# Fused attention and gated FFN block in fp32 on one core: late weights loaded behind the first move of queries, the planner's view of an x load in pieces, and the last pair's norm on ACT and DVE

## The chip, the cores and the metric

One core of a Trainium2 chip runs the whole kernel. The metric is the device time of one execution in microseconds; the figure of a kernel is the median of its runs. The engines are TensorE (PE: matmuls, and transposes done as matmuls), VectorE (DVE), ScalarE (ACT), GpSimd (POOL) and SyncE (SP). SP issues nearly all DMAs here, in order: an issue that waits holds up all behind it. An L with a number is a line of the kernel before.

## What is computed

x has 4096 rows of 256 numbers, all fp32. A block of windowed attention (16 query heads in 4 groups, head size 16, each row sees the 128 rows up to itself) and a gated feed-forward block (with a mix of each row and the row before it) follow each other, each with a residual and a layer norm:

```python
q = x @ Wq + bq;  k = x @ Wk + bk;  v = x @ Wv + bv      # k, v: 4 groups of 16
mask = (i - 128 >= j) | (i < j)
att = softmax(where(mask, -1e9, q @ k.T / sqrt(16)))
x = layernorm(x + (att @ v) @ Wo + bo)
x_prev = concat([0, x[:-1]])
xr = mu_r * x + (1 - mu_r) * x_prev
xk = mu_k * x + (1 - mu_k) * x_prev
r = sigmoid(xr @ W_r.T);  k = xk @ W_k.T
out = r * (square(relu(k)) @ W_v.T)
x = layernorm(x + out)
```

## The kernel before, in words

**Tiling.** The rows are 32 blocks of 128. Two blocks are a pair p (16 pairs), four blocks a chunk c (8 chunks of 512 rows). Projections run by chunk, attention and feed-forward by pair. x is wanted with its columns on the partitions. For pairs 0 to 3 x is loaded as it is (256 KB, L439) and turned on PE; from pair 4 on it is loaded in four pieces of 64 KB (`load_x_turned`, L453) laid out so that DVE can turn it in squares of 32 (L459). Buffer ring `x` has four places, so pair 4 takes that of pair 0.

**Before the loop.** The function first issues, on SP, x of pairs 0 and 1, Wk, Wv, Wq, x of pairs 2 and 3, then the weights of the feed-forward block W_k, W_r, W_v (L481), Wo in four parts (L502), bo (L507), and mu_r and mu_k (L527). Then come constants and the first transposes of x on PE (L619).

**Attention.** For a chunk: `kv` (L730), two query products `q` (L778) with a copy each on ACT (L789), and `q move` (L800): four DMAs from SBUF to SBUF that bring the odd heads' queries to the partitions of the even ones. All score products read what it moves. `vT` (L753) transposes the values; `ones` (L764) is a small DMA that fills rows of kT. For a pair: `maxima` (L855 with masks L833 and L842) are score products of which DVE takes row maxima (L865); these are turned and sent by four small DMAs (`nm put`, L879) into the queries; `weights a` and `weights b` (L942 with masks L914, L928) are the score products anew, transposed, with the maximum subtracted, and ACT takes their exponentials (L979, L1013); `values` (L1040, L1053) multiplies with v; then `wo` (L1180), the addition of the residual `xres` (loaded in L1165, bo added on POOL in L1171), and the norm.

**Feed-forward.** `fk` (L1296), relu on ACT (L1306), square on POOL (L1310), `fr` (L1323) with the gate on ACT (L1337), `fv` (L1323), then the gating product (L1350), the residual (L1355) and the norm: bn_stats and bn_aggr on DVE (L1118, L1119), four small operations on POOL for the scale (L1124 to L1130), apply on ACT (L1136). The last pair, 15, goes in two halves of 128 rows (`plan_last`, L1383 to L1419): product, gating, residual, statistics and apply on DVE, the power that gives the scale on POOL (L1409). The residual addition of pair 14 is on DVE, of the others on POOL.

**What sets the order.** All operations behind the prologue go through `Plan`. `op` records engine, length, a rank (the kind's own from the table `KINDS`, plus a base that grows with the pair) and what is read and written; `run` then simulates all engines with these lengths and writes the instructions out in the order of the simulated starts. On each engine it takes, among the operations that could start within 0.35 of the earliest, that with the lowest rank. PE is an exception: the table `ORDER` fixes its list by position (0, 1, 2, ...), whatever the simulation says. In it the transposes of W_k, W_r and W_v (`w`, L666) stand at positions 29, 30 and 10. What the prologue loads enters the plan as `given`, of no length, with a landing time written by hand; `begin sp` and the like stand for the prologue's own time on each engine. `QUEUE` holds the time a kind takes of the DMA queue in the simulation. The planner's figures set the order alone; on the chip an instruction starts when its semaphores allow.

In the simulation the four pieces of an `x load` share a buffer, so pieces 1 to 3 depend on piece 0, the taker of the buffer:

```python
deps.update(self.taker[k] for k in uses if k in self.taker)
```

and they could start only when it had landed in the simulation. On the chip they write different partitions and don't wait for each other.

Of the kernel before, what the change touches and what calls it, by code (L numbers as in the profile page):

```python
# [8 lines left out]
F32 = mybir.dt.float32  # L9
# [11 lines left out]
P = 128  # L21
NG = 4
# [16 lines left out]
    "begin pool": (POOL, 5.3, -536.56),  # L39
    "begin sp": (SP, 8.0, -360.66),  # L40
    "w": (PE, 0.43, 0),
    "w copy": (ACT, 0.62, 0.22),
    "x load": (SP, 0.5, -0.16),
    "x turn": (DVE, 0.7, 28.13),
# [43 lines left out]
    "y2 last": (DVE, 0.42, -24.81),  # L88
    "stats last": (DVE, 1.1, 59.97),
    "scale last": (POOL, 0.8, -21.85),  # L90
    "apply last": (DVE, 0.46, -51.24),
    "fv": (PE, 1.72, 0),
# [13 lines left out]
QUEUE = {  # L106
    "x load": 0.45, "x1 in": 0.45, "q move": 1.6, "xres": 1.3, "x1 out": 1.3, "store": 1.3,
}
# [103 lines left out]
class Plan:  # L212
# [20 lines left out]
    def op(self, kind, base, fn, r=(), w=(), uses=(), new=(), banks=(), mode=None, late=None):  # L233

        i = len(self.ops)
        eng, length, rank = KINDS[kind]
        n = self.count[kind] = self.count.get(kind, -1) + 1
        rank = ORDER[kind][n] if eng == PE and ORDER else rank + base  # L240
        deps = set()
        for k in r:
            if k in self.writer:
                deps.add(self.writer[k])
            self.readers.setdefault(k, []).append(i)
        for k in w:
            if k in self.writer:
                deps.add(self.writer[k])
            deps.update(self.readers.pop(k, ()))
            self.writer[k] = i  # L250
        deps.discard(i)
        for k in list(uses) + [key for _, key in new] + [key for key, _ in banks]:
            self.users.setdefault(k, []).append(i)
        deps.update(self.taker[k] for k in uses if k in self.taker)
        for ring, key in new:
            self.taker[key] = i
            ring.queue.append(key)
        for key, _ in banks:
            self.taker[key] = i
        if late is None:  # L260
            late = self.LAND if eng == SP else 0.0
        self.ops.append((eng, length, rank, fn, deps, list(new), list(banks), mode, late, QUEUE.get(kind, 0.1 if eng == SP else 0.0)))

# [3 lines left out]
    def run(self):  # L267
# [42 lines left out]
        while cand:  # L310
# [24 lines left out]
            cand.remove(i)  # L335
            eng, length, _, fn, _, new, banks, mode, late, q = ops[i]
            for ring, key in new:
# [14 lines left out]
            for k in nexts[i]:  # L352
                hop = 0.0 if ops[k][0] == eng and not late else self.DRAIN if eng == PE else self.HOP
                if ops[k][0] == PE and eng == PE:
                    hop = 0.0
                ready[k] = max(ready[k], end[i] + hop)
                left[k] -= 1
                if not left[k]:
                    cand.add(k)
# [7 lines left out]
def postln_block(  # L367
# [63 lines left out]
    def ring(tag, bufs=2):  # L431
        return rings.setdefault(tag, Ring(bufs))
# [63 lines left out]
    ffn_l = {"r": wl_r, "k": wl_k, "v": wl_v}  # L496
    for k, w in (("k", W_k), ("r", W_r), ("v", W_v)):
        load_w(ffn_l[k], w)

    wo = const.tile([P, 2, D], F32, tag="wo", name="wo")  # L500
    for g in range(NG):
        nc.sync.dma_start(  # L502
            out=wo[32 * g : 32 * (g + 1), :, :],
            in_=Wo[64 * g : 64 * (g + 1), :].rearrange("(rp x) n -> x rp n", x=32),
        )
    bo_b = const.tile([P, D], F32, tag="bo_b", name="bo_b")
    nc.sync.dma_start(out=bo_b, in_=bo.partition_broadcast(P))  # L507

# [4 lines left out]
    vecs = const.tile([P, NV], F32, tag="vecs", name="vecs")  # L513
    muT = const.tile([P, 2, C2], F32, tag="muT", name="muT")
    with nc.allow_non_contiguous_dma(reason="small vectors, once"):
# [5 lines left out]
        for o in range(2):  # L521
# [3 lines left out]
            )  # L525
        for w, mu in enumerate((mu_r, mu_k)):
            nc.sync.dma_start(out=muT[:, w, :], in_=mu.rearrange("(p c) -> p c", c=C2))  # L527

# [153 lines left out]
    def plan_load(p):  # L682
# [4 lines left out]
        else:  # L687
            op("given", p, lambda: None, w=[("x", p)], new=[(ring("x", 4), ("x", p))], late=(3.7, 4.5, 7.0, 7.8)[p])

# [598 lines left out]
    def plan_k(p, base):  # L1288
# [19 lines left out]
        def square():  # L1308
            kact[p] = sb.tile([P, C2, H2], F32, tag="kact", name=f"kact_{p}")
            nc.gpsimd.tensor_tensor(kact[p].rearrange("p o n -> p (o n)"), st["kr"], st["kr"], ALU.mult)  # L1310

        op("fk", base, product, r=[("xm", 1, p, 0), ("xm", 1, p, 1), ("w", "k")], w=[key], uses=[("xmt", 1, p)], new=[(ring("kr"), ("krt", p))], banks=[(key, 1)], mode="full")
        soon = base - (60 if p == NP - 1 else 0)
        op("relu", soon, relu, r=[key], w=[("kr", p)], uses=[key, ("krt", p)])
        op("square", soon, square, r=[("kr", p)], w=[("kact", p)], uses=[("krt", p)], new=[(ring("kact"), ("kactt", p))])

# [59 lines left out]
    def plan_last(p, b, base):  # L1376
# [14 lines left out]
        def gated():  # L1391
# [3 lines left out]
            nc.vector.scalar_tensor_tensor(y, sig[p][:, b, :], 1.0, bank(key)[:, 0:D], ALU.add, ALU.mult)  # L1395

        def rest():
            y = y2s[p][:, b, :]
            nc.vector.tensor_tensor(y, y, x1[p][:, b, :], ALU.add)
# [3 lines left out]
            nc.vector.bn_aggr(st["mv"], s6)  # L1403
            nc.vector.tensor_scalar(st["mv"][:, 1:2], st["mv"][:, 1:2], EPS, None, ALU.add)

        def scale():
            ve = st["mv"][:, 1:2]
            st["rstd"] = small.tile([P, 1], F32, tag="rstd_last", name=f"rstd_last_{b}")
            nc.gpsimd.tensor_tensor(st["rstd"], ve, nhalf[:, 0:1], ALU.pow)  # L1409

        def apply():
            if not b:
                res[p] = sb.tile([P, 2, D], F32, tag="res", name=f"res_{p}")
            nc.vector.tensor_scalar(
                res[p][:, b, :], y2s[p][:, b, :], st["mv"][:, 0:1], st["rstd"], ALU.subtract, ALU.mult
            )
# [9 lines left out]
        op("y2 last", base, gated, r=[key, ("sig", p)], w=[("y2a", p, b)], uses=[key, ("sigt", p), y2t])  # L1426
        op("stats last", base, rest, r=[("y2a", p, b), ("x1", p, b)], w=[("y2", p, b)], uses=[y2t, ("x1t", p)])
        op("scale last", base, scale, r=[("y2", p, b)], w=[("rstd", p, b)])
# [7 lines left out]
    for p in range(NP):  # L1436
        c, h = divmod(p, 2)
        plan_load(p)
        if p == 1:
            for k, t in (("k", 9.5), ("r", 10.5), ("v", 11.3), ("wo", 12.0), ("bo", 12.5), ("mu", 13.5)):  # L1440
                op("given", 0, lambda: None, w=[("rest", k)], late=t)
            op("given", 0, lambda: None, w=[("wq",)], late=7.4)
# [13 lines left out]
        plan_v(c, b0)  # L1456
        if c == 0:
            for i, (k, scale) in enumerate((("k", 1.0), ("r", 1.0), ("v", 0.5))):
                plan_weight(k, i, scale)
# [54 lines left out]
```

## Time and profile before

| | us |
|---|---|
| median of 3 runs (345.37 to 349.35) | 346.02 |
| the profiled execution, device time | 345.45 |
| its span, first to last instruction | 343.7 |
| mean granted clock of TensorE | 0.986 |
| first real product (L778) starts | 6.83 |
| last matmul ends | 336.7 |
| last apply on DVE ends (L1414) | 340.80 |
| last store issued on ACT's queue (L1419) | 340.84 |

A line of the chain gives start, duration, engine and line of the work that ended last, followed back from the end; SPq is SP's queue issuing a DMA. A line of the timeline gives start, duration, engine, line, operation, output and inputs, and the number of instructions. A line of a stretch gives PE's busy time, the clock it was granted (1.00 is full), the mean share of the 16 DMA engines that was busy, and GB/s. The waits name who waited for what: total us, times, longest.

### The profile page before, as it was taken

To read this page: it belongs to the slowest core of one execution; us is meant where nothing else is said; L and a number is where in the kernel's file an instruction comes from. 1 tells how busy PE (TensorE), PEld (TensorE's weight loads), DVE (VectorE), ACT (ScalarE), POOL (GpSimd) and SP (SyncE) were. 2 spreads that over 40 slices of the span, in tenths; PEclk is the share of its full clock that TensorE was granted. 3 is DMA by queue.
4 is the path that set the end of the run, shared out by engine and by line. 5 is a ranking of instruction groups with operands and counts; after the bars stand their busy time and mean duration, and the time that the engine had idled before them with its cause. 6 is when DMAs were issued, how large, how long until landed. Compare 5 with 4: busy or idle time off the path is not lost.

```text
span 343.7 us, 11149 instructions
## 1 busy us (share of the span) xinstructions
PE 331.5 (96%) x4729; PEld 221.7 (64%) x4729; DVE 268.9 (78%) x494; ACT 165.8 (48%) x227; POOL 124.8 (36%) x220
## 2 busy tenths in 40 slices
PE   8899999999999999999999999999999999999991
PEld 6455566655765676567666656767767676678871
DVE  7067787778888859999789998698948897678675
ACT  2402554556337583272442645653762386834541
POOL 5200000111404334161326231427632765648773
PEclk9969999999999999999999999999999999999998
DMA  6842333121511243211123220322221224210002
GB/s 191 226 100 47 75 78 68 35 67 19 139 33 35 69 89 94 67 33 58 42 60 98 63 68 32 65 82 84 55 87 41 65 70 120 79 49 31 32 31 92
DMA packets 55062, 24.65 MB, mean 72 GB/s; under 512 B 40644, under 2 KB 54852, under 8 KB 55012
## 3 DMA queue, kind: packets, MB, share of 16 engines
q1 hardware_dynamic: 54832, 23.81, 26.3%
q8 instruction: 37, 0.61, 0.8%
q10 hardware_dynamic: 180, 0.13, 0.1%
q14 instruction: 13, 0.11, 0.1%
HBM read 13.64 MB, written 7.86 MB: 63 GB/s over the span
## 4 chain that ended last, share of the span: by engine, by line
PE 83%; DVE 7%; SPq 3%; POOL 2%; issue 1%; DMA 1%; ACT 1%; POOLq 0%; DVEq 0%
PE ps L1323 14%; PE ps L942 12%; PE ps L855 9%; PE ps L1040 8%; PE ps L1180 8%; PE ps L778 8%; PE ps L1296 7%; PE ps L1053 4%; PE ps L730 4%; PE ps L842 2%; PE ps L914 2%; DVE xm L1268 2%; SPq L800 2%; DVE nm L865 1%; PE ps L753 1%
## 5 line engine op out<-in xcount | busy, mean ns | idle before, releaser
L865 DVE TENSOR_REDUCE nm<-ps 128x6 f32<-128x960 f32 (+1 forms) x96 | 94.7, 1037 | 16.6 <-PE ps L855 15.0
L979 ACT ACTIVATE prA<-ps 128x1024 f32<-128x1024 f32 x64 | 63.2, 1024 | 56.7 <-PE ps L914 53.1
L942 PE MATMUL ps<-qT,kT 17*64 17x512 f32 (+1 forms) x1024 | 54.7, 499 | 0.0
L855 PE MATMUL ps<-kT,qT 16*128 16x160 f32 x1024 | 48.8, 309 | 2.4 <-DMA qT<-qT 2.3
L1124 POOL TENSOR_SCALAR ve_y<-mv_y 128x2 f32<-128x2 f32 x31 | 8.0, 257 | 96.2 <-DVE mv_y L1119 95.3
L855 PEld LDWEIGHTS ps<-kT,qT 16*128 16x128 f32 x1024 | 39.5, 188 | 4.6 <-DMA qT<-qT 3.3
L1268 DVE SCALAR_TENSOR_TENSOR xm<-xd,muT,x1T 128x256 f32<-128x256 f32 x64 | 36.1, 614 | 5.4 <-POOL xd L1260 4.3
L1013 ACT ACTIVATE prB<-ps 128x1024 f32<-128x1024 f32 x32 | 31.0, 1021 | 13.7 <-PE ps L914 12.7
L1260 POOL TENSOR_TENSOR xd<-x1T 128x512 f32<-128x512 f32 x16 | 16.6, 1040 | 43.8 <-DVE x1T L459 43.8
L1065 DVE STREAM_TRANSPOSE oN<-ps 128x1024 f32<-128x1024 f32 x16 | 20.0, 1248 | 15.5 <-PE ps L1053 15.4
L1180 PE MATMUL ps<-wo,attT 128*128 128x256 f32 x128 | 31.4, 388 | 0.3 <-ACT prA L979 0.2
L778 PE MATMUL ps<-xT,wq 128*128 128x512 f32 x64 | 31.2, 612 | 0.3 <-DVE wq L631 0.3
L1040 PE MATMUL ps<-prA,vA 128*32 128x256 f32 x512 | 30.9, 382 | 0.4 <-ACT prA L979 0.2
L1296 PE MATMUL ps<-xm,wkT 128*128 128x256 f32 x128 | 30.8, 383 | 0.0
L1323 PE MATMUL ps<-wrT,xm 128*128 128x256 f32 x128 | 30.8, 383 | 0.0
L1118 DVE BATCH_NORM_STATS2 st_y<-y 128x6 f32<-128x256 f32 x62 | 25.3, 408 | 6.2 <-POOL y L1355 5.6
L942 PEld LDWEIGHTS ps<-qT,kT 17*64 17x64 f32 x1024 | 19.6, 130 | 15.5 <-issue 7.7
L1355 POOL TENSOR_TENSOR y<-y,x 128x512 f32<-128x512 f32 x14 | 19.1, 1364 | 28.0 <-DVE y L1350 27.9
L1323 PE MATMUL ps<-wvT,kact 128*128 128x256 f32 x120 | 29.0, 385 | 0.2
L1171 POOL TENSOR_TENSOR xres<-xres,bo_b 128x512 f32<-128x512 f32 x16 | 20.3, 1271 | 23.1 <-DMA xres<-in_L_attn_x 20.1
L1323 PEld LDWEIGHTS ps<-wrT,xm 128*128 128x128 f32 x128 | 23.8, 190 | 5.2 <-issue 1.6
L1180 PEld LDWEIGHTS ps<-wo,attT 128*128 128x128 f32 x128 | 23.3, 190 | 4.9 <-ACT prA L979 1.1
(109 smaller groups left out, 478.1 us busy)
## 6 DMA issues: line engine op xcount, KB each, us to landing
xres<-in_L_attn_x SPq DMA_DIRECT2D x16, 256.0 KB
out<-res SPq DMA_DIRECT2D x15, 256.0 KB
x1d<-x SPq DMA_DIRECT2D x14, 256.0 KB
x1w<-x1d SPq DMA_DIRECT2D x56, 64.0 KB
x<-in_L_attn_x SPq DMA_DIRECT2D x48, 64.0 KB
qT<-qT SPq DMA_DIRECT2D x32, 64.0 KB
x<-in_L_attn_x SPq DMA_DIRECT2D x4, 256.0 KB
qT<-nmT SPq DMA_DIRECT2D x64, 4.0 KB
```

Of the source, the lines that this page charges most:

```text
L778: nc.tensor.matmul(ps, wq[:, ch, rp, :, :].rearrange("p g x -> p (g x)"), xT[c][:, ch, :], start=(ch == 0), stop=(ch == C2 - 1),)
L855: nc.tensor.matmul(sc[g // 2][:, g % 2, u * W : (u + 1) * W], qT[c][g0 : g0 + DH, (2 * p + j) % NB, s, :, :, :].rearrange("p o r i -> p (o ...
L865: nc.vector.tensor_reduce(nms[p % 2].rearrange("p g j s -> p g (j s)")[:, 2 * i : 2 * i + 2, lo:hi], two_banks(keys[i])[:, :, 0 : n * W].r ...
L942: nc.tensor.matmul(dst[g], kT[k, k0 : k0 + 64], qT[c][k, blk, r0 : r0 + nr, :, :, :].rearrange("p s o r i -> p (s o r i)"), start=start, s ...
L979: nc.scalar.activation(prA[b][:, 2 * i : 2 * i + 2, :], two_banks(keys[i]), AF.Exp)
L1013: nc.scalar.activation(prB[p][:, 2 * i : 2 * i + 2, :, :].rearrange("p g j n -> p g (j n)"), two_banks(keys[i]), AF.Exp,)
L1040: nc.tensor.matmul(av[32 * g : 32 * (g + 1), hf, j, :], vA[:, values_of(b, g)], prA[b][:, g, hf * H : (hf + 1) * H], start=(j == 0), stop= ...
L1118: nc.vector.bn_stats(s6, src()[:, b, :])
L1180: nc.tensor.matmul(ps[:, j, :], attT[2 * p + j][:, rp, :, :].rearrange("p s i -> p (s i)"), wo[:, rp, :], start=(rp == 0), stop=(rp == 1),)
L1268: nc.vector.scalar_tensor_tensor(dst[p][:, ch, :], st["d"][:, ch, :], muT[:, which, ch : ch + 1], x1T[p][:, ch, 0:H2], ALU.mult, ALU.add,)
L1296: nc.tensor.matmul(ps[:, o, :], ffnT["k"][:, ch, o * P : (o + 1) * P], xk[p][:, ch, :], start=(ch == 0), stop=(ch == C2 - 1),)
L1323: nc.tensor.matmul(ps[:, b, :], lhs[:, ch, b * P : (b + 1) * P], w[:, ch, :], start=(ch == 0), stop=(ch == C2 - 1),)
```

## The change

Three edits.

1. **Late weights.** W_k, W_r, W_v, wo, bo and mu are no longer loaded in the prologue. They become operations of the plan on SP that read both copies of the first chunk's queries, as the first `q move` does. Their rank is that of chunk 0, above the move's and below that of all further x loads. `begin sp` goes from 8.0 to 5.2, and the landings of x of pairs 2 and 3 from 7.0 and 7.8 to 7.5 and 8.5. The order of the loads among themselves, PE's list and the ranks of all other kinds stay.
2. **Pieces of an x load.** Where one SP operation depends on another only as the taker of a buffer, the simulation lets it start when the other has been issued.
3. **The last pair.** Its square goes from POOL to DVE, with a rank of its own. For its first half the residual addition also gives the row sum; a small DVE operation makes the negative mean of it; ACT squares what is centred with the sum over the row; POOL makes the variance of it, then the power; apply adds the negative mean in place of subtracting the mean. The second half keeps its operations.

```diff
-    "begin sp": (SP, 8.0, -360.66),
+    "begin sp": (SP, 5.2, -360.66),
+    "rest": (SP, 0.5, 0),
+    "rest wo": (SP, 1.8, 0),
+    "rest bo": (SP, 0.4, 0),
+    "rest mu": (SP, 0.7, 0),
...
-    "stats last": (DVE, 1.1, 59.97),
+    "add last": (DVE, 0.52, -24.81),
+    "squares last": (ACT, 0.6, -60),
+    "stats last": (DVE, 1.1, -24.81),
+    "square last": (DVE, 0.75, -60),
...
-        deps.update(self.taker[k] for k in uses if k in self.taker)
+        takers = {self.taker[k] for k in uses if k in self.taker} - deps
+        soft = {d for d in takers if eng == SP and self.ops[d][0] == SP}
+        deps |= takers
...
-                ready[k] = max(ready[k], end[i] + hop)
+                ready[k] = max(ready[k], s + length if i in ops[k][10] else end[i] + hop)
...
-    for k, w in (("k", W_k), ("r", W_r), ("v", W_v)):
-        load_w(ffn_l[k], w)
...
+    def load_late(k):
+        if k in ffn_l:
+            load_w(ffn_l[k], {"r": W_r, "k": W_k, "v": W_v}[k])
+        elif k == "wo":
...
-            op("given", p, lambda: None, w=[("x", p)], new=[(ring("x", 4), ("x", p))], late=(3.7, 4.5, 7.0, 7.8)[p])
+            op("given", p, lambda: None, w=[("x", p)], new=[(ring("x", 4), ("x", p))], late=(3.7, 4.5, 7.5, 8.5)[p])
...
-            nc.gpsimd.tensor_tensor(kact[p].rearrange("p o n -> p (o n)"), st["kr"], st["kr"], ALU.mult)
+            (nc.vector if p == NP - 1 else nc.gpsimd).tensor_tensor(kact[p].rearrange("p o n -> p (o n)"), st["kr"], st["kr"], ALU.mult)
...
+        def add():
+
+            y = y2s[p][:, b, :]
+            total = small.tile([P, 1], F32, tag="sum_last", name=f"sum_last_{b}")
+            nc.vector.scalar_tensor_tensor(y, y, 1.0, x1[p][:, b, :], ALU.mult, ALU.add, accum_out=total)
+            st["nmean"] = small.tile([P, 1], F32, tag="nmean_last", name=f"nmean_last_{b}")
+            nc.vector.tensor_scalar(st["nmean"], total, -1.0 / D, None, ALU.mult)
+
+        def squares():
...
+            nc.scalar.activation(
+                own, y2s[p][:, b, :], AF.Square, bias=st["nmean"], accum_out=st["ssq"]
+            )
...
+            if not b:
+                nc.gpsimd.tensor_scalar(st["ve"], st["ssq"], 1.0 / D, EPS, ALU.mult, ALU.add)
...
-            for k, t in (("k", 9.5), ("r", 10.5), ("v", 11.3), ("wo", 12.0), ("bo", 12.5), ("mu", 13.5)):
-                op("given", 0, lambda: None, w=[("rest", k)], late=t)
...
+            for k in ("k", "r", "v", "wo", "bo", "mu"):
+                op("rest " + k if len(k) > 1 else "rest", 0, lambda k=k: load_late(k), r=[("qe", 0, 0), ("qe", 0, 1)], w=[("rest", k)])
```

## The prediction

> **What bounds the kernel now.** The page first: TensorE (PE) is busy nearly throughout, and its granted clock dips once, in the third of 40 slices.
>
> ```profile
> PE 331.5 (96%) x4729; PEld 221.7 (64%) x4729; DVE 268.9 (78%) x494; ACT 165.8 (48%) x227; POOL 124.8 (36%) x220
> PEclk9969999999999999999999999999999999999998
> ```
>
> PE runs one fixed list, so what is lost on it early stays lost, and what is won early carries to the end. Of 343.7 us it idles 12.2: 1.1 before its first matmul, some 4 between 15.5 and 20, 7.0 behind its last matmul (336.7). Next the chain of waits at the start (start, us, what):
>
> ```profile
> 6.83 3.70 PE ps L778 x8
> 10.53 0.96 PE ps L698 x8
> ...
> 14.72 0.75 SPq L800
> ...
> 16.81 2.68 DMA qT<-qT
> ...
> 20.60 1.60 PE ps L855 x21
> 22.20 1.05 PE ps L666 x4
> 23.25 3.41 PE ps L730 x4
> ```
>
> The chain leaves PE at one place: the first move of queries (L800, four DMAs). Its input, the second copy of queries on ACT, is ready at 11.26 (the timeline has 10.57 + 0.69), but SP, whose queue is in order, issues it at 14.72, behind 24 loads. The fourth piece lands at 16.81 + 2.68 = 19.49 and PE goes on at 19.53. Then the granted clock (stretch: us, PE busy, PEclk, DMA share, GB/s):
>
> ```profile
> 16.00:17.00 1.00, 0.00 (x0) 1.00 0.63 138
> 19.00:20.00 1.00, 0.78 (x14) 1.00 0.74 167
> 20.00:21.00 1.00, 1.00 (x28) 0.68 0.49 108
> 21.00:27.00 6.00, 6.00 (x34) 0.50 0.43 97
> 27.00:28.00 1.00, 1.00 (x29) 0.91 0.64 147
> ```
>
> Behind the stall the clock is halved for some 7 us; the four L730 matmuls took 3.41 there, and 1.72 at 41.21. SP's own waits between 8 and 30 us show why it is late:
>
> ```profile
> SPq L453 <- DMA wl_kact<-in_L_ffn_W_v: 0.5, 1, 0.5
> SPq L527 <- DMA wl_xr<-in_L_ffn_W_r: 0.5, 1, 0.5
> SPq L507 <- DMA x<-in_L_attn_x: 0.4, 1, 0.4
> SPq L527 <- DMA wl_xr<-in_L_ffn_W_k: 0.3, 1, 0.3
> ```
>
> Each is a wait for the DMA issued eight before on SP: bo (8.79) for x of pair 3, the two mu (9.48, 10.35) for W_k and W_r, the first x piece (11.30) for W_v. So W_k, W_r, W_v land at about 9.45, 10.3 and 11.25. Last the end, on DVE and POOL:
>
> ```profile
> 333.63 1.04 POOL L1310 TENSOR_TENSOR kact<-kr 128x512 f32<-128x512 f32 x1
> ...
> 333.65 1.57 DVE L1355 TENSOR_TENSOR y<-y,x 128x512 f32<-128x512 f32 x1
> ...
> 338.43 0.42 DVE L1399 TENSOR_TENSOR y<-y,x 128x256 f32<-128x256 f32 x1
> ```
>
> From 332.92 DVE is busy without a gap until 339.72; the last scale on POOL, the last apply (340.39 + 0.41 = 340.80) and the store follow.
>
> **The head, step by step.** Removed ahead of the loop: ten issues on SP, from 4.96 to 10.68. What SP issues next is set by the planner's rule (earliest start, lowest rank within 0.35): with pieces that no longer wait for each other I get both xres, four pieces of x 4, four of x 5, one of x 6, then the query move, then W_k, W_r, W_v, ones, wo, bo, mu, then the rest of x 6 and 7. Times, at 0.47 an issue as in the rows: xres 4.96 and 5.47; they queue behind x of pair 3 (landed by 8.75) as W_k and W_r did, so land at about 9.5 and 10.3. Pieces of x 4 go from 5.95 to 7.9, of x 5 from 7.95 to about 10.8, held up by the eight-ahead rule (for x 3 at 8.75, xres at 9.5 and 10.3). The piece of x 6 overwrites x 2, which PE reads in L698 until about 10.95, so issues at 11.0 to 11.45. The move then starts at about 11.5 for 14.72: **3.2 us earlier**. Its four issues took 2.70 and the fourth landed 2.68 after its issue; the same from 11.5 gives 16.3. PE reaches this point at 15.35 as before (L753), so 4 us of stall become about 1.
>
> That holds if the eight pieces of x 4 and 5, 512 KB issued before it, are through. 1 KB rows moved at up to 379 GB/s (9 to 10 us); these pieces, with short rows, at 147 (27 to 28, at 0.64 of the engines), so 230 if saturated: my estimate, 512 KB in 2.3 us behind 10.3, 12.6, against a first piece due at 14.1. At 147 it is 13.9: still in time, barely.
>
> **The clock.** From 19.53 to the query product at 28.04 the chain is PE alone, 8.51 us, with 0.32 + 3.0 + 0.09 = 3.4 lost to the clock by the rows above. With about 1 us of idle (15.35 to 16.3) in place of 4 I take it that the clock stays up: 5.1 us instead, **3.4 won**. The nearest rows: the 0.3 us gap at 6.5 left the clock at 1.00; behind PE's last matmul it fell only at about 341.2, after 4.5 us of idle. Bounds: 0 to 3.4.
>
> The Trainium skill (TensorE: Matmul & The Clock Gate, Part 1) halves the clock after one idle window of some 3.4 us. Here it fell though the record has PE 53 to 78% busy from 17 to 20, on a few thin matmuls, so the page's idle must mean low activity; by its window alone a 1 us stall costs nothing, and by the row a half-busy one could.
>
> **The added wait.** W_v is transposed tenth on PE's list (L666, at 22.14 now, long after landing); W_k and W_r only at 49.06, wo at 62.98, mu later still, so those are hidden. W_v is now the third weight behind the move: W_k issued at 14.2, W_v at 15.2. An xres issued at 12.17 let POOL go at 15.24, 3.0 us; the two 256 KB loads directly ahead take 0.85 each by the landings above but start 0.5 apart, which adds some 0.3: 18.5. PE gets there at 16.3 + (22.20 - 19.53 = 2.67, less 0.92 of clock) = 18.05. **Cost 0.45.** Lower bound 0 (landing 2.6 after issue, as the query pieces); upper bound from W_v itself, 5.99 to 11.25 = 5.3 us on a full queue: landing 20.5, cost 2.4. I take the xres row, since the queue is then about as full. Everything behind it on PE waits with it: the second L730, then all score products. DVE behind: four L865 took 3.90 from 20.14; from 16.9 they end at 20.8, when PE wants their banks: 0.1.
>
> Other things moved: bo now lands near 21, so POOL's L1171 (15.24 now) slips by 6 us; its reader is the addition behind wo at 62.98, cover of 40 us, and without it the 6 us would be paid. The rest of x 6 and 7 issue by about 23 (27.35 now); used from 37.26. The next query move is issued at 33.01 now, behind nothing that moved.
>
> Head: 3.2 + 3.4 - 0.45 - 0.1 = 6.05.
>
> **The tail.** The last square leaves POOL. Its 1.04 ran beside DVE's addition, which took 1.57; two-input 128x256 took 0.42, so 128x512 alone is some 0.7 to 0.8 (L1190: 0.68 with one input in PSUM). DVE saves 0.85. The square costs DVE 0.7, in the gap and statistics between 331.3 and 332.9, where it idles 0.8 for PE. PE need not wait for kact: 0.2. For the first half of the last pair, bn_stats, bn_aggr and the epsilon (0.43 + 0.18 + 0.15) leave DVE for a 0.15 scaling; the sum rides on the addition, up to 0.15 more for reading it out. ACT's square (0.6) and POOL's 0.22 + 0.55 run while DVE does the second half. New sequence on the old clock: addition 333.65 to 334.35, statistics to 335.54, half 0 from 335.7 (PE at 334.53 + 1.0 and drain) to 336.85, half 1 gate and statistics (0.41 + 1.29) to 338.6, POOL 0.6, apply to 339.7 for 340.80: **1.1 won**. If the gate waits behind ACT's apply, or ACT has to load a table (1.28 at 3.49), 0.3; if accumulation is free, 1.4.
>
> Against it, the Trainium skill (SBUF — State Buffer, two separate sides) has a DVE operation with two SBUF inputs and a GpSimd operation shut each other out; both new DVE operations are such, beside POOL's scale. By the page up to 0.7 goes; the rows disagree for small ones: the 0.42 addition at 338.43 ran beside POOL's 0.55 (338.18) undelayed.
>
> **The sum.** 6.05 + 1.1 = 7.15. The profiled execution took 345.45 (span 343.7 and 1.75 around it), 0.57 under the median 346.02: 345.45 - 7.15 = **338.3**. PE's list, ranks and loops between are the same, so I put nothing there.
>
> **Rivals.** (1) The clock falls all the same, since 16 to 18.5 has two stalls with thin matmuls between: 3.4 back, 341.7. For it: the dip came with PE half busy by the record. Against: under 1.5 of any 3.4 us would be idle. (2) The move goes early but lands late, x pieces being slow or SP held by the eight-ahead rule until they land: 1.5 lost, 339.8. For it: 147 GB/s; against: the queue then has no W_k to W_v. The extreme, an order with all of x 6 first, adds 1.4: the change would hardly do what it says. (3) Slower: PE's list still has W_v tenth. If W_v lands late, PE stands with all of the list behind it and the clock falls as before. Each us is a us; break-even with the old exit is a landing at 22.2, with the tail's 1.1 at 23.3, and over 2% slower (6.9) needs 30.2. At 24.5, 346.6. Against: 5.3 us is the longest landing in the rows, which is 20.5 (340.2, or up to 343.6 with the clock).
>
> **Chances.** Forecast 0.67, own range 337 to 340; (1) 0.14; (2) 0.13; (3) 0.06. The range 336.5 to 342.3 takes in the better tail and clean landings (7.15 + 0.45 + 0.1 + 0.3 = 8.0, and 1 for the unseen middle), and (1) and (2). Two per cent, about what a measurement here can tell from no change, lies at 339.1: three quarters of the forecast and a little of (2) are faster, 0.52; slower 0.04, most of (3) being less; same 0.44.
>
> **What would show it.** L800 first issued near 11.5 and its DMA ending near 16.3; PEclk 9 in slice three; the second L730 near 1.7 us; L666 starting near 18.5 with a DMA as its releaser; DVE's L1355-like addition near 0.7; end 1 us closer to the last matmul. Wrong if the clock dips, if L800 stays near 14, or if a gap opens between 30 and 325.

## The result, and the profile after

| | before | after |
|---|---|---|
| median, 20 runs of each on one chip | 345.75 us (344.48 to 349.35) | 342.24 us (340.09 to 344.39) |
| ratio | 1 | 0.9884, 95% interval 0.9863 to 0.9904 |
| profiled execution: device time, span | 345.45, 343.7 | 343.44, 341.7 |
| first query product starts | 6.83 | 7.08 |
| second query product starts | 28.04 | 27.53 |
| last query product starts | 211.56 | 210.85 |
| last apply ends | 340.80 | 338.79 |

The change won 3.5 us, 1.2%, where 7.15 was forecast (338.3). 342.24 lies at the upper edge of the range, 0.06 inside it. The profiled execution is one of the longer ones of its kernel, 1.2 above its median; that matters below. Lines of the code stand 10 further down than before at the loads, 15 from the transposes to the norm: L463 is an x piece, L491 a load of W_k, W_r or W_v, L681 their transposes (L666 before), L745 `kv`, L768 `vT`, L793 `q`, L815 the query move (L800), L870 `maxima` (L855), L957 `weights`.

The page of the kernel after, busy time by engine and the granted clock in 40 slices:

```profile
PE 328.6 (96%) x4729; PEld 220.1 (64%) x4729; DVE 265.6 (78%) x494; ACT 165.7 (48%) x229; POOL 124.1 (36%) x220
PEclk9969999999999999999999999999999999999999
```

The digit of the third slice was to become 9. It is 6, the same as before. PE's waits in the first 60 us say what stands in the place of the stall for queries (total us, times, longest):

```profile
PE ps L681 <- DMA wl_kact<-in_L_ffn_W_v: 3.1, 1, 3.1
...
PE ps L870 <- DMA qT<-qT: 0.2, 1, 0.2
```

The same view of the kernel before has, for the moved queries:

```profile
PE ps L855 <- DMA qT<-qT: 2.3, 3, 1.8
```

The stall for the moved queries is nearly gone: 0.2 us as one wait, where the kernel before has 2.3 in three. Behind it PE waits 3.1 us for W_v, a wait that the kernel before did not have. The chain of waits at the start (start, duration, what):

```profile
12.47 0.40 SPq L815
...
16.04 5.73 DMA wl_kact<-in_L_ffn_W_v
21.91 1.08 PE ps L681 x4
23.00 3.41 PE ps L745 x4
...
27.53 1.91 PE ps L793 x4
```

The query move is on the chain no longer than to its issues; then come the three loads behind it on SP, of which W_v, issued last at 16.04, lands 5.73 later at 21.77. Four L745 then take 3.41 us, the duration of L730 before, because the clock is halved. PE by stretches (us, PE busy, clock, DMA share, GB/s):

```profile
18.00:19.00 1.00, 0.82 (x22) 1.00 0.87 292
19.00:20.00 1.00, 0.00 (x0) 0.80 0.73 211
...
22.00:26.00 4.00, 4.00 (x8) 0.50 0.41 90
```

So in this execution one stall was exchanged for another, with the clock halved behind it as before, and the head won 0.5 us (28.04 to 27.53). The clock did not wait for the end of the stall: PE stops at 18.82, and 0.80 between 19 and 20, with 1.00 ahead and 0.50 behind, puts the fall at about 19.6, some 0.8 us into it. The last rows of DVE's timeline (in brackets the idle time ahead and what ended it), which answer to the tail:

```profile
331.07 0.66 DVE L1325 TENSOR_TENSOR kact<-kr 128x512 f32<-128x512 f32 x1
...
332.60 0.69 DVE L1370 TENSOR_TENSOR y<-y,x 128x512 f32<-128x512 f32 x1
...
334.98 0.42 DVE L1410 SCALAR_TENSOR_TENSOR y<-sig,ps 128x256 f32<-128x256 f32 x1 [0.49 <-ACT sig L1352]
...
338.38 0.41 DVE L1452 TENSOR_SCALAR res<-y,mv_last,rstd_last 128x256 f32<-128x256 f32 x1 [0.23 <-POOL rstd_last L1447]
```

The addition takes 0.69 in place of 1.57, the square 0.66 on DVE. The gate of the first half (334.98) waits for `sig`. The chain that ended last shows what is behind that wait:

```profile
331.24 0.57 POOL ve_y L1139
...
334.47 0.49 ACT sig L1352
```

From the start of the last query product to the end of the last apply it is 129.24 us before and 127.94 after: 1.3 nearer.

### The profile page after: what moved, and what is told of

Read it like the earlier page. It is cut to its first block, busy times and chain, and to the rows that moved or that the text cites. A ratio compares the mean times of both kernels' runs of the same rounds, so it can differ in the third digit from the quotient of the medians.

```text
span 341.7 us, 11147 instructions
## 1 busy us (share of the span) xinstructions
PE 328.6 (96%) x4729; PEld 220.1 (64%) x4729; DVE 265.6 (78%) x494; ACT 165.7 (48%) x229; POOL 124.1 (36%) x220
## 4 chain that ended last, share of the span: by engine, by line
PE 88%; DMA 3%; DVE 3%; ACT 2%; issue 1%; SPq 1%; POOL 1%; POOLq 0%; DVEq 0%; ACTq 0%
PE ps L1338 15%; PE ps L957 14%; PE ps L870 10%; PE ps L1055 9%; PE ps L793 8%; PE ps L1195 8%; PE ps L1311 8%; PE ps L1068 5%; PE ps L745 4%; PE ps L857 2%; PE ps L929 2%; DMA wl_kact<-in_L_ffn_W_v 2%; PE ps L768 1%; DMA wl_xk<-in_L_attn_Wq 1%; ACT prA L994 1%
## 5 line engine op out<-in xcount | busy, mean ns | idle before, releaser
L880 DVE TENSOR_REDUCE nm<-ps 128x6 f32<-128x960 f32 (+1 forms) x96 | 94.8, 1038 | 18.0 <-PE ps L870 16.7
L957 PE MATMUL ps<-qT,kT 17*64 17x512 f32 (+1 forms) x1024 | 54.3, 499 | 0.0
L870 PE MATMUL ps<-kT,qT 16*128 16x160 f32 x1024 | 47.0, 305 | 0.3 <-DMA qT<-qT 0.2
L870 PEld LDWEIGHTS ps<-kT,qT 16*128 16x128 f32 x1024 | 38.0, 185 | 2.7 <-issue 1.4
L1283 DVE SCALAR_TENSOR_TENSOR xm<-xd,muT,x1T 128x256 f32<-128x256 f32 x64 | 33.5, 570 | 5.9 <-POOL xd L1275 4.4
L793 PE MATMUL ps<-xT,wq 128*128 128x512 f32 x64 | 31.2, 612 | 0.8 <-DVE wq L646 0.8
L957 PEld LDWEIGHTS ps<-qT,kT 17*64 17x64 f32 x1024 | 19.6, 130 | 15.1 <-issue 7.7
L1275 POOL TENSOR_TENSOR xd<-x1T 128x512 f32<-128x512 f32 x16 | 16.7, 1045 | 33.3 <-DVE x1T L469 33.1
```

Of the source, the lines that this page charges most:

```text
L793: nc.tensor.matmul(ps, wq[:, ch, rp, :, :].rearrange("p g x -> p (g x)"), xT[c][:, ch, :], start=(ch == 0), stop=(ch == C2 - 1),)
L870: nc.tensor.matmul(sc[g // 2][:, g % 2, u * W : (u + 1) * W], qT[c][g0 : g0 + DH, (2 * p + j) % NB, s, :, :, :].rearrange("p o r i -> p (o ...
L880: nc.vector.tensor_reduce(nms[p % 2].rearrange("p g j s -> p g (j s)")[:, 2 * i : 2 * i + 2, lo:hi], two_banks(keys[i])[:, :, 0 : n * W].r ...
L957: nc.tensor.matmul(dst[g], kT[k, k0 : k0 + 64], qT[c][k, blk, r0 : r0 + nr, :, :, :].rearrange("p s o r i -> p (s o r i)"), start=start, s ...
L1283: nc.vector.scalar_tensor_tensor(dst[p][:, ch, :], st["d"][:, ch, :], muT[:, which, ch : ch + 1], x1T[p][:, ch, 0:H2], ALU.mult, ALU.add,)
```

## The experiments

Theory A: the head's gain is real and sized about as forecast, and W_v's place behind the move takes most of it back, by the wait and by the clock that falls behind it. Rivals: the clock falls whatever PE waits for; the load queue as such is what counts; the gain is all the tail's.

One table for all, from the profiled executions, in us; "last q" is the start of the last query product, a mark behind which only the tail differs. The ratio is to runs of the kernel before on the same chip.

| kernel | second q | last q | last apply ends | median | ratio, 95% interval |
|---|---|---|---|---|---|
| before | 28.04 | 211.56 | 340.80 | 345.75 | 1 |
| after | 27.53 | 210.85 | 338.79 | 342.24 | 0.9884 (0.9863 to 0.9904) |
| W_v first | 21.59 | 206.34 | 334.28 | 338.98 | 0.9802 (0.9774 to 0.9829) |
| W_v first, more runs | 21.79 | 206.88 | 334.82 | 339.95 | 0.9845 (0.9814 to 0.9877) |
| W_v second | 24.37 | 207.59 | 335.52 | 340.31 | 0.9850 (0.9828 to 0.9872) |
| W_v turned late | 21.29 | 208.74 | 336.68 | 341.41 | 0.9871 (0.9832 to 0.9910) |
| W_v in the prologue | 22.59 | 207.49 | 335.42 | 340.31 | 0.9876 (0.9812 to 0.9940) |
| filler ahead of W_v | 27.13 | 210.02 | 337.96 | 340.98 | 0.9853 (0.9817 to 0.9889) |
| pieces wait again | 32.55 | 217.97 | 345.83 | 350.51 | 1.0122 (1.0075 to 1.0168) |
| old end | 25.72 | 208.84 | 337.82 | 342.34 | 0.9909 (0.9883 to 0.9934) |
| before, new end alone | 28.11 | 211.04 | 339.37 | 344.20 | 0.9950 (0.9931 to 0.9969) |
| before, pieces alone | 30.52 | 213.96 | 342.95 | 346.34 | 1.0023 (1.0000 to 1.0047) |
| before, stall filled | 26.93 | 210.46 | 339.35 | 343.21 | 0.9948 (0.9913 to 0.9984) |
| W_v first, stall filled | 23.47 | 207.98 | 335.93 | 339.38 | 0.9808 (0.9782 to 0.9834) |

### W_v first behind the move

```diff
-            for k in ("k", "r", "v", "wo", "bo", "mu"):
+            for k in ("v", "k", "r", "wo", "bo", "mu"):
```

> The changed kernel with one edit: W_v is the first of the three late weights, not the third. Theory A (W_v's landing holds PE at its transposes, L681, for 3.1 us in the changed kernel's profile, and that hold brings the clock down): W_v is issued near 14.9 in place of 16.04, lands near 18, PE gets there at 18.8, so the wait is under 0.3; the clock stays at 1.00 and the first-chunk products behind it (L745, 3.41 us) take 1.7; some 6 us won, 0.975 to 0.982 of the kernel before. Rival B (the clock falls anyway, from the thin score products at 15.5 to 18.8): wait gone, L745 still 3.4, 0.982 to 0.985. Rival C (what is won at the head is given back later): wait and dip gone, yet 0.988.

The chain of waits of this kernel:

```profile
13.53 2.76 DMA qT<-qT
...
18.16 0.59 PE ps L681 x4
18.75 1.72 PE ps L745 x4
...
29.53 3.59 DMA qT<-qT
...
33.16 0.81 PE ps L870 x10
```

PE comes to W_v's transposes with no wait, four L745 take 1.72, the clock is 1.00 in all stretches from 16 to 28. The second query product starts 6.45 us earlier than before. Only the order of three loads differs from the kernel after. PE's waits from 20 us on are these:

```profile
PE ps L870 <- DMA qT<-qT: 0.5, 1, 0.5
...
PE ps L957 <- issue: 0.4, 1, 0.4
```

Both lie between 28 and 34 us, and the chain there runs through the second query move (its last piece lands at 29.53 + 3.59 = 33.12). The kernel before has no wait there, and at the last query product 5.22 of the 6.45 are left. This is what is late next once the head is won. The ratio lies in A's range; of the 6 us that A named over the kernel after, the second query product shows 5.9, the medians 3.3.

### W_v second

```diff
-            for k in ("k", "r", "v", "wo", "bo", "mu"):
+            for k in ("k", "v", "r", "wo", "bo", "mu"):
```

> The kernel after with W_v loaded second behind the move (order W_k, W_v, W_r). Theory A (the loss grows with W_v's landing, and each place further back in the queue costs): W_v is issued at 14.7 to 15.5 and lands between the 18.1 of the first place and the 21.8 of the third, near 19.5; PE waits 0.5 to 1.5 us for it, the clock may or may not fall behind that; 339.5 to 341 (ratio 0.982 to 0.986). Rival B (only the third of three such loads is late, by something that strikes the last one): W_v lands by 18.7, no wait, as with W_v first, 339 (0.980).

The chain of this kernel:

```profile
15.10 4.01 DMA wl_kact<-in_L_ffn_W_v
19.25 1.09 PE ps L681 x4
20.34 2.92 PE ps L745 x4
```

W_v lands at 19.11, PE waits 0.8 for it, and L745 takes 2.92 for 1.72 with the clock halved from about 19.2 (0.60 from 19 to 20, 0.50 behind). The second query product (24.37) lies between that of the first place (21.59) and that of the third (27.53), and landing, wait and time lie in A's ranges; W_v as second is not free in this execution. That each place back costs is not shown by the times: the ratio's interval overlaps that of the longer series with W_v first (0.9814 to 0.9877) and that of the kernel after.

### W_v turned late

PE's list with the transposes of W_v at place 28 (what stood at 11 to 28 moves up by one); loads as in the kernel after.

```diff
-        29, 30, 10,
+        29, 30, 28,
```

> The kernel after, with the transposes of W_v at place 28 of PE's list in place of 10 (what stood at 11 to 28 moves up by one); the loads stay in the order W_k, W_r, W_v. Theory A (all of the missing gain is PE standing for W_v's landing at 21.8 us, and the halved clock that follows that stand): W_v is wanted only near 45 us, so PE has no wait for it, four L745 matmuls take 1.7 us in place of 3.41, the clock stays at 1.00 between 17 and 30, and the time is that of the run with W_v loaded first, 339 (ratio to before 0.980, 0.977 to 0.983). Rival B (W_v loaded first helped because the load queue behind the move changed, not because PE was let go): no gain over the kernel after, 341.5 to 342.5 (0.987 to 0.990).

The head did what A says: no wait for W_v, the second query product at 21.29 (without the 0.59 of the transposes ahead of it). The time did not: 341.41, near what B forecast. In the profiled execution the clock fell later, between 34 and 39 us, behind the pauses at the second query move, on this part of the chain:

```profile
35.33 1.05 PE ps L768 x4
36.37 2.80 PE ps L745 x4
```

These take 0.59 and 1.72 with W_v first: 1.5 us lost in these two rows. So it is not enough to let PE go: the clock can fall later as well. That the pauses brought it down is not shown, since with W_v first nearly the same pauses stand there (PE busy 0.68 from 32 to 33 us; 0.70 here) and the clock stayed at 1.00. One of the four runs had a mean clock of 0.998 and yet took 341.48; that is not explained, as the only profile is of another run.

### W_v in the prologue

```diff
+    load_w(wl_v, W_v)
...
-            for k in ("k", "r", "v", "wo", "bo", "mu"):
+            for k in ("k", "r", "wo", "bo", "mu"):
```

> The kernel after, with W_v alone loaded ahead of the loop (behind x of pair 3) as in the kernel before; W_k, W_r, wo, bo and mu stay behind the move. Theory A: W_v costs one issue of 0.5 us on SP and 256 KB of the queue ahead of the x pieces, the query move goes some 0.5 to 0.8 us later than in the kernel after (12.6 to 12.9 for 12.13), no wait for W_v, clock 1.00: 339 to 340 (ratio 0.980 to 0.984). Rival B (each load ahead of the move holds it up by its whole landing, through the wait of an issue for the one eight before): the move goes near 14 again, the clock dips in the query stall, 342 or more (0.989 and up).

The query move went at 12.37, earlier than A allowed for, and no wait for W_v was left; the clock was 1.00 from 14 to 100. Three of four runs took 340.07 to 340.41, the fourth 344.81 at a mean clock of 0.979, which makes the interval wide. The median lies just beyond A's range and the ratio further, and the move did not go near B's 14. A load of 256 KB ahead of the x pieces costs about 1 us of the head (22.59 against 21.59).

### Filler ahead of W_v's transposes

48 bf16 matmuls of a constant tile, in the place where PE waits for W_v. They add work and leave the output as it is.

```diff
+            if k == "v":
+                for _ in range(48):
+                    nc.tensor.matmul(bank(key)[:, 0:P], filler, filler, start=True, stop=True)
```

> The changed kernel with 48 small bf16 matmuls put on PE directly ahead of W_v's transposes, where PE idles 3.1 us; nothing else. It parts the two prices of the hold, standing time and clock. Theory A: the hold itself stays (L681 starts near 21.8), the clock stays at 1.00 behind it, L745 takes 1.7 and not 3.4, some 2.5 to 3.4 us less than the changed kernel, 0.979 to 0.982 of the kernel before. Rival B (the dip doesn't come from idling at W_v): L745 3.4 still, 0.988 or, if the fillers cost time, 0.990.

In the profiled execution the clock fell before the fillers could help: 0.69 from 19 to 20, with PE busy in all of 18 to 19, behind pauses of 0.3 and 0.3 us in the query stall (16 to 17.1). The fillers then took 4.38 us at half clock and brought it back, so that the four L748 (`kv`) took 1.72. The second query product came no earlier than 27.13. Two of the four runs had a mean clock of 0.998 and took 340.0 and 340.2, two 0.989 and took 341.75 and 342.6. Neither expectation held as written: L745 was short, as A said, but the ratio lies between the two. The wait for W_v can't be the only thing that lowers the clock.

### The pieces wait again

The second edit undone, the rest as after:

```diff
-        soft = {d for d in takers if eng == SP and self.ops[d][0] == SP}
+        soft = set()
```

> The changed kernel with its second edit undone: in the plan the pieces of an x load wait for the first one's landing again. If the second edit is of no weight: five x pieces rather than nine stand ahead of the first query move, which goes near 11.6, W_v with it 0.5 us earlier, and the time is 0.985 to 0.990 of before. If it is what brings the query move forward: the move goes at 14 or later and the time is 0.993 to 1.000.

Both expectations fell. The move went earlier (10.83), since the plan now puts the pieces of x 5 behind the weights (SP issues them from 20.63), and PE's waits show the price:

```profile
PE ps L793 <- DVE xT L469: 3.3, 1, 3.3
PE ps L681 <- DMA wl_kact<-in_L_ffn_W_v: 2.8, 1, 2.8
```

The second query product stands for x, behind a wait for W_v nearly as long as in the kernel after (here W_v takes 5.50 from 14.74). 350.51: with the first edit alone in the head the kernel is slower than before, and the second edit is worth some 8 us beside it.

### The second edit alone

The kernel before, with the second edit (the lines of the change's diff on `takers` and `ready`).

> The kernel before, with the second edit alone (pieces of an x load don't wait for each other in the plan). Theory A (the second edit matters only since the weights are gone from the prologue; with them there the pieces of x 4 and 5 are issued ahead of the move as before): 345.0 to 346.5, ratio 0.998 to 1.002. Rival B (it is worth as much by itself as with the first edit, where its undoing cost 8 us): 338 to 343, ratio under 0.992. A loss, if more pieces now go ahead of the move and delay it: up to 348.

346.34, the interval from 1.0000 to 1.0047. The first x piece goes only at 12.17, when W_v has landed (5.92 + 6.17 on the chain), all eight pieces of x 4 and 5 then go ahead of the move, and that is issued at 16.05 in place of 14.72. By itself the edit is worth nothing or slightly less: the loss that the expectation named third, but a small one.

### The new end alone, and the old end

The kernel before with the third edit alone:

> The kernel before with the third edit alone (last pair's norm on ACT and DVE, its square on DVE). Theory: it is worth what the two profiles show behind the last shared matmul, about 1.05 us (the forecast had 1.1): 0.996 to 0.998 of before. Rival: it is worth nothing by itself, since the store of pair 14 or the DMA behind the end sets the time: 0.999 to 1.001.

The kernel after without its third edit:

> The kernel after with the last pair as before (square on POOL, both halves with bn_stats): the first two edits alone. Theory A (the tail's edit is worth what the profiles of before and after give from the last query product to the last apply, 129.24 and 127.94, 1.3 us, and what the edit alone gave, 1.7): 343.5 to 344 (ratio to before 0.992 to 0.995). Rival B (with the head gained, the tail's gain is lost or doubled): 342.3 or 345.

Alone it won 0.5% (1.7 us, interval 1.1 to 2.4), more than the theory's 0.2 to 0.4%. Undone in the kernel after it cost 0.25% by the ratios (0.9909 against 0.9884, 0.9 us; the two intervals overlap), and nothing by the medians (342.34 against 342.24, on different chips), which is the lower number of rival B. The times don't decide. The profiles are sharper: from the start of the last query product to the end of the last apply it is 127.93 to 127.95 in the eight profiles with the first two edits and the new end, and 128.98 in that with the old end: 1.04 us. (The other profiles with the old end have 129.24 before, 128.99 with the pieces alone and 128.89 with the stall filled; with the new end alone it is 128.33, where the pieces wait 127.86.)

The old-end run gave more than it was made for. Here W_v, in the third place as in the kernel after, landed 3.45 us behind its issue at 16.05 (5.73 in the other profile), and PE waited only 0.4 for it. Yet the clock fell, and before that wait. Its stretches, then PE's timeline there (start, duration, engine, line, operation; in brackets the idle time ahead and what ended it; L867 is L870 of the kernel after, L678 its L681):

```profile
17.00:18.00 1.00, 1.00 (x27) 1.00 1.03 346
18.00:19.00 1.00, 1.00 (x22) 0.63 1.03 350
19.00:20.00 1.00, 0.60 (x3) 0.50 0.52 162
```
```profile
15.04 1.67 PE L867 MATMUL ps<-kT,qT 16*128 16x160 f32 x6
17.00 0.67 PE L867 MATMUL ps<-kT,qT 16*128 16x160 f32 x9 [0.29 <-DMA qT<-qT]
...
19.64 0.66 PE L678 MATMUL ps<-ident,wl_kact 128*128 128x128 f32 x2 [0.40 <-DMA wl_kact<-in_L_ffn_W_v]
```

PE is busy in all of 17 to 19, and the clock goes down within 18 to 19, ahead of the wait for W_v. Ahead of it lie a pause of 0.29 at 16.7 and thin score products (16 of 128 rows), and there the record's busy time says more than was done: the first six products are spread over 1.67 us, as the moved queries land in pieces (PE's weight loads wait for them 1.1 us in three times), where the next nine take 0.67. With W_v first the six take 0.64 and 0.84, the weight loads wait 0.6 once, and the clock stayed up in both profiles. But such waits alone don't settle it: with W_v in the prologue they are 1.2 in three, and the clock stayed up too.

### The query stall of the kernel before, filled

The kernel before with 56 short bf16 matmuls ahead of its first score products. They add work and leave the output as it is.

```diff
+            if p == 0 and unit == 2:
+                for _ in range(56):
+                    nc.tensor.matmul(sc[0][:, 0, 0:P], filler, filler, start=True, stop=True)
```

> The kernel before, with 56 short bf16 matmuls on PE (of a constant tile into a bank of the scores, overwritten afterwards) ahead of the first score products, where PE stands for the moved queries from 15.5 to 19.5 us. They add work of some 4 to 5 us in a stretch of 4 us of idle. Theory A (the halved clock between 20.3 and 27 us comes of PE's standing still and costs 3.4 us): clock 1.00 from 19 to 30, four L730 in 1.7 us in place of 3.41, and 342 to 343.5 (ratio 0.988 to 0.993; the fillers may end up to 1 us behind the landing of the queries). Rival B (the clock falls by something else, such as the load of the first stretch or a fixed time after the start): dip as before, 346 to 347 (1.000 to 1.003).

0.9948: about half of what A gave by its ratio, though the median, 343.21, is among A's times. In the profiled execution the fillers ended at 18.4, PE stood 0.94 for the queries still, and the clock fell later and for less long (0.67, 0.50, 0.50, 0.62 in the four stretches from 22 to 26). The ten runs sort themselves: mean clock 0.992 to 0.996, six runs, 342.04 to 343.52; 0.986 and 0.987, two runs, 346.26 and 346.66; two lie between, 0.990 and 0.991 at 345.29 and 343.99, the second being the profiled one. Between the outer groups lie some 3.8 us (342.63 and 346.46 in the middle): an estimate of the price of a long fall, close to the 3.4 worked out in the prediction from durations.

### W_v first, more runs, and with the stall filled

> The kernel after with W_v loaded first behind the move, the same kernel as in the first experiment, over more runs. If its gain is the order of the loads: 338.8 to 339.5, ratio to before 0.979 to 0.983, its interval wholly below that of the kernel after (0.9863 to 0.9904). If the first measurement was a lucky phase of the clock: 340 to 342.

339.95, between the two expectations, and a ratio whose interval (0.9814 to 0.9877) overlaps that of the kernel after: the first measurement was in part lucky. The six runs: 338.57 to 340.41 at mean clocks of 0.994 to 0.996, four of them; 341.47 and 341.92 at 0.984 and 0.988. The ten runs of both rounds together have a median of 339.25, 3.0 under the kernel after; by the ratios, each to the kernel before on its own chip, it is 2.8 and 1.3 us. Then the same kernel with 14 fillers (0.8 us) where PE stands for the queries:

```diff
+            if p == 0 and unit == 2:
+                for _ in range(14):
+                    nc.tensor.matmul(sc[0][:, 0, 0:P], filler, filler, start=True, stop=True)
```

> The kernel after with W_v loaded first behind the move, and 14 short bf16 matmuls (59 ns each in the earlier filled run, 0.8 us in all) ahead of the first score products, so that PE hardly stands for the moved queries between 15.3 and 16.6. In the ten runs with W_v first the mean clock was 0.994 or more in seven, 0.984 to 0.989 in three, at 340.3 to 341.9 in place of 338.6 to 340.4. Theory A (the pauses of 0.3 to 0.7 us in that stall are what lets the clock fall in some runs): 0.993 or more in every run, median 338.8 to 339.3. Rival B (the thin score products themselves are as good as a pause to the clock, or the fall lies elsewhere): 0.984 to 0.989 in about a third of the runs, median 339 to 340.

339.38, clocks 0.991 to 0.998, five of the six at 0.994 or more. Neither expectation held to the letter: no run as low as B's 0.984 to 0.989, one below A's 0.993. Filling the pause may make the fall rarer (one of six against three of ten); six runs don't show it. By its median W_v first beats both kernels in every set of runs, and its filled form is no faster than it. (In the filled form's profile the first eight query products took 5.59 for 3.71 at a granted clock of 1.00, ahead of all that differs; that is not explained.)

## Why the prediction was right and wrong

That the time lies in the range is luck in part. The upper end, 342.3, was set so as to take in rival (1), the gain is about half of the forecast, and by the prediction's own signs it was wrong: the clock dipped.

**The added wait: the step that failed.** It took W_v's landing from a load of xres, 3.0 us behind its issue and 0.3 more, cost 0.45. Measured: 5.73 and a wait of 3.1 in the profile of the kernel after, 3.45 and 0.4 in that with the old end, 5.50 and 2.8 where the pieces wait. W_v's own row of before, 5.3, stood in the text as the upper bound and is near two of the three: it is a 256 KB load behind two others of 256 KB, while xres had had x pieces ahead of it. The reason given, that the queue is then about as full, compared fill and not what stood ahead. That this is the cause is argued, not shown: with the old end the same loads stood ahead, and the landing and the wait were those of the forecast. What it costs without a fall can be estimated from the runs at a mean clock of 0.993 or more, though these are on different chips and only two of them have a profile: 340.5 in the middle of four with W_v third, 338.96 in the middle of seven with W_v first, 1.5 apart.

**The clock.** It was sized well (3.4; some 3.8 between the runs of the filled kernel), but put down as won. In the profile of the kernel after the fall cost less, some 2.2 by the rows (half of the time from 21.9 to 26, and 0.2 behind it), since PE stood through its first part. In all four profiles with W_v third and the pieces not waiting (after, old end, filler, turned late) the clock fell somewhere between 18 and 39 us, and so it did with W_v second; in the four with W_v first or in the prologue it did not. The 20 runs of the kernel after have mean clocks from 0.979 to 0.996, four at 0.993 or more; of the ten with W_v first, seven. So the fall goes with the place of W_v, but these are single profiles, and it also comes with W_v first in some runs. The named fall-back "the clock falls all the same", 341.7, is the nearest to 342.24. Its mechanism, two stalls with thin matmuls between, is not quite what the old-end profile shows, where the clock fell ahead of the second stall; that of the slower rival, PE standing for W_v with the clock falling as before, is what the profile of the kernel after shows. Both were listed, and both were held too unlikely together. The prediction also read the old stall as some 4 us of idle time; by its own rows PE idles 2.4 between 15 and 20, and the rest of the 4 is the thin products spread through it.

**The query move, 3.2 us earlier.** It is issued at 12.13 in the profile after (2.6 earlier) and at 11.44 with W_v first (3.3), where the last piece lands at 13.53 + 2.76 = 16.29; 11.5 and 16.3 were forecast, and SP's order came as forecast. Right with W_v first. In the profile after, Wq landed at 6.77 and the first product started 0.25 later, which is part of the difference. With the old end the first product started earlier (6.52), and the move went at 12.14 all the same: there the second xres, put at about 10.3, landed at 5.34 + 5.88 = 11.22 and held SP's last pieces.

**The head as a sum.** Without the 0.45 it was 6.5 forecast, and 6.45 and 6.25 with W_v first at the second query product: right. It does not carry through. "The next query move is issued at 33.01 now, behind nothing that moved" saw the queue, but not that PE, 6 us earlier, now waits for this move itself: 5.22 and 4.68 are left at the last query product. This term, 1.2 and 1.6 in the two profiles, was missing.

**What was said to be hidden** was: POOL adds bo to xres only at 22.91, and its reader at 62 does not wait. DVE's 0.1 does not show.

**The tail, 1.1.** 1.04 by the profiles with the same head. The addition 0.69 (0.7), the square 0.66 (0.7). The risk that the gate stands behind ACT came true in part: the first half's gating product waits 0.49 for `sig`, which ACT computes behind two applies of pair 14. On the shared lock, the Trainium skill (SBUF — State Buffer, two separate sides) is borne out by these rows: the addition took 1.57 beside POOL's square (333.63 to 334.67) and takes 0.69 without it, and POOL's scaling of two numbers, 0.22 in the old end, takes 0.57 beside DVE's new square, and its last step 0.49 for 0.20 beside the addition. The price of up to 0.7, which the sum left out, fell on POOL, and it was not covered: the chain runs from there through the applies of pair 14 on ACT to `sig` and to the gate that waits. The first half's gate was forecast at 335.7, which is 334.99 with the head's 0.71 off, for PE's sake; it came at 334.98, for ACT's. The 1.1 is right by luck there.

**The clock and the page.** The Trainium skill (TensorE: Matmul & The Clock Gate, Part 1) has a free-running window, so that the same kernel meets it at another phase from run to run. The spread of the mean clock, 0.979 to 0.996 in one kernel, agrees. Its rule of an idle window of some 3.4 us does not describe what was measured: in the old-end execution the clock fell with PE busy by the record for all but some 0.4 of the 3 us before, and with no more than six thin products from 15.04 to 16.71. By the page alone, the forecast would have kept the clock there.

**Open.** Why the same load in the same place lands 3.45 us after its issue in one execution and 5.73 in another, and what the clock weighs beside PE's pauses: no run tells the thin score products from the pauses between them, and none parts them from the chance of one execution.

## What to carry to other kernels

When loads are moved behind something urgent, look up who reads each first on an engine with a fixed list, and send the first one needed first: here the order of three loads was worth some 2 to 3 us, nearly as much as the change. Take the landing of a load from the row that has the same loads ahead of it, and allow for its spread. And follow a gain to the next transfer of the same kind: an engine that comes 6 us earlier waits at the next move.

## What the runs showed of the hardware

Two things were not expected. The clock fell where PE's longest pause in the 3 us before was 0.29 us (old end), and the mean clock differs between executions of one kernel (0.979 to 0.996), so a profile of one execution is a sample: that of the kernel after lies 1.2 us above its median, and its wait of 3.1 is not the wait of every run. And the third of three 256 KB loads issued within 1.2 us of each other landed 3.45 us after its issue in one profile and 5.3 to 6.17 in the others that show it, the second 4.01.
